# Cross-attention with image prompts: context transposed by VectorE in squares of 32, prompt keys as four columns behind the text keys

## The chip, the cores and the metric

The kernel runs on one core of a Trainium2 chip. TensorE (PE) multiplies, VectorE (DVE) and ScalarE (ACT) read TensorE's results out of PSUM, GpSimd (POOL) works on SBUF, and SyncE (SP) issues most DMAs. The metric is the device time of one execution in microseconds; less is better. All data are float32.

## What is computed

Eight batches, each with S = 112 query rows of 320 channels (20 heads of 16) and a context of 375 rows of 512 embedding values. The first 371 rows are text tokens, the last 4 are image prompt tokens. Cut to what matters:

```python
q   = heads(x @ W_q)                       # 112 x 16 for each of 20 heads
k_t = heads(text @ W_k);  v_t = heads(text @ W_v)
probs_t  = softmax(q k_t^T * 0.25)          # 112 x 371
text_out = probs_t v_t
k_ip = heads(ip @ W_k_ip); v_ip = heads(ip @ W_v_ip)
attn = q k_ip^T * 0.25                      # 112 x 4, the prompt logits
qsem = l2norm(probs_t text)                 # 112 x 512 for each head
sem  = qsem l2norm(ip)^T                    # 112 x 4
probs_ip = softmax(attn + 0.5 * sem) * mask
out = (text_out + probs_ip v_ip) @ W_out + b_out + x
```

The kernel does not form qsem. It uses the Gram matrix of the context: with p the unnormalised probabilities of a head, p (text text^T) p^T gives the norm, and p (text ip^T) the similarities. So for each head it multiplies p by a matrix that has the Gram columns of the 371 text tokens, then 4 columns for the prompts, a column of ones and the 16 value columns: 392 columns in all.

## The kernel before

**Steps.** The 20 heads of a batch are five groups of four. The main loop runs over 40 steps (b,g), batch b and group g. The order of work on TensorE, VectorE, ScalarE and SP is the order of the program text, written out by hand; GpSimd's is left to a scheduler (it is in text order too in the last batch). Within step n:

- `multiplied` (L631): 12 blocks of 32 tokens, each with 4 matmuls (one for a head, in the four row groups of the array) into four PSUM banks ps_qd; since the Gram matrix is symmetric each block is 32 columns narrower than the one before, 392 down to 40.
- `scores` (L584) of step n + 2 (LEAD = 2): two heads after the first block, two after the seventh. They lie in the two PSUM banks ps_s of the pool ps_sc.
- `probabilities` of step n + 2: the row maximum on VectorE (L597, nmx), the exponential on ScalarE (L601, p), and a DMA that puts p into the tile xg (L604).
- `transposed` of step n + 1, after block 2: one VectorE instruction that transposes xg in squares of 32 (L612, xgT). `multiplied` of the next step reads xgT.
- behind the last block: `value_sums` on ScalarE (L644), the maxima of the last two heads, `reduced` on VectorE (L677, four reductions that read the four ps_qd banks), `placed` on GpSimd (L553, value columns into the matrix u of the next step), and then `between`.

**Work between steps.** `between(b, g)` prepares batch b + 1 (and the context of b + 2) a piece at a time: `gram` at g = 0 (L411), `values` at g = 1 and 2 (L480), `keys` block 0 at g = 2 and blocks 1 and 2 at g = 3 (L447; block 2 is a transpose of columns that came with the values, L438), `project_queries` of a pair of batches (x transposed at L295, matmuls L303, then qm = query times a mask on VectorE L312, and qT = a plain copy on ScalarE L315), `finish` of batch b - 1 in ten pieces.

**The context.** `load_ctx` fetches 375 x 512 into the tile ct, token by partition, in four DMAs (L129, L131), at the end of step (b,0) for batch b + 2. `transposed_context` turns it in `between(b, 4)` for batch b + 2: 12 TensorE transposes (L353) into ps_c and three ScalarE copies (L363) into ctxT, which holds embedding by partition and is read by `gram`, `values` and `keys`. The embedding index is e * 128 + p: chunk e, partition p. The weights W_k, W_v, W_k_ip and W_v_ip are loaded in the same order by `load_embed` (L115).

**The prompts' logits.** `prompt_projections` makes kip (keys of all 32 prompt tokens) and from it kipb (L256), each key once for every head of its block with the other heads' channels at zero, for all batches. `prompt_logits(b)` multiplies qT by kipb (L564, three matmuls) in `between(b, 3)`, for the last batch after its step 0, and ScalarE copies the result to ipl (L571), which `finish` reads (L746).

Of the kernel before, what the change touches and what calls it, by code (L numbers as in the profile page):

```python
# [8 lines left out]
F32 = mybir.dt.float32  # L9
# [5 lines left out]
NIP = 4  # L15
# [5 lines left out]
def kernel(  # L21
# [34 lines left out]
    SCALE = D ** -0.5  # L56
    N = B * NIP

    GROUP = 4
    NG = H // GROUP  # L60
    BLK = TP // RG
# [50 lines left out]
        eng.dma_start(t[:REST, FULL, :C], w[FULL * P :, :])  # L112

    def load_embed(eng, t, w):
        eng.dma_start(t[:, :, :C], w.rearrange("(e p) f -> p e f", p=P))  # L115

    def spread(eng, t):

# [2 lines left out]
            eng.tensor_copy(v[:, :, a, 0, :], v[:, :, a // 2, a % 2, :])  # L121
        eng.memset(v[:, :, :, 1, :], 0.0)

    def load_ctx(b):
        ct = io.tile([P, NT, E], F32, tag="ct", name=f"ct_{b}")
        for c in range(NT):
            rows = min(P, T - c * P)
            some = rows - rows % 16
            nc.sync.dma_start(ct[:some, c, :], ehs[b, c * P : c * P + some, :])  # L129
            if some < rows:  # L130
                nc.sync.dma_start(ct[some:rows, c, :], ehs[b, c * P + some : c * P + rows, :])  # L131
        return ct
# [62 lines left out]
    kipb = const.tile([P, NC, B, HC, NIP], F32, tag="kipb", name="kipb")  # L195
# [17 lines left out]
    def normalised_prompts():  # L213

        sq = work.tile([N, E], F32, tag="ipn", name="ipsq", bufs=1)
        ss = small.tile([N, 1], F32, tag="ipss", name="ipss", bufs=1)
        nc.vector.tensor_tensor_reduce(
            out=sq, in0=ip_sb, in1=ip_sb, scale=1.0, scalar=0.0, op0=ALU.mult, op1=ALU.add,
            accum_out=ss,
        )  # L220
        nc.vector.tensor_scalar_max(ss, ss, EPS * EPS)
        rn = small.tile([N, 1], F32, tag="iprn", name="iprn", bufs=1)
        nc.scalar.activation(rn, ss, AF.Sqrt)
        nc.vector.reciprocal(rn, rn)

        ipn = work.tile([N, E], F32, tag="ipn", name="ipn", bufs=1)
        nc.vector.tensor_scalar(ipn, ip_sb, rn, 0.5, op0=ALU.mult, op1=ALU.mult)
        yield

        for src, dst, n in ((ipn, ipnT, "n"), (ip_sb, ipT, "r")):  # L230
            ps = bank(f"ps_ipT{n}")
            for e in range(NE):
                nc.tensor.transpose(
                    ps[:, e * N : (e + 1) * N], src[:, e * P : (e + 1) * P], ident[:N, :N]
                )
            nc.vector.tensor_copy(
                dst, ps[:, : NE * N].rearrange("p (e n) -> p e n", n=N)
            )
        yield

    def prompt_projections():

        spread(nc.gpsimd, wkip_sb)
        for i in range(NC):
            ps = bank(f"ps_kip{i}")
            for e in range(NE):
                nc.tensor.matmul(
                    ps[:, :N],
                    wkip_sb[:, e, i * P : (i + 1) * P],
                    ipT[:, e, :],  # L250
                    start=(e == 0),
                    stop=(e == NE - 1),
                )
            kip = work.tile([P, N], F32, tag="kip", name=f"kip_{i}")
            nc.scalar.copy(kip, ps[:, :N])
            nc.vector.tensor_tensor(  # L256
                kipb[:, i],
                kip.rearrange("p (b n) -> p b n", n=NIP).unsqueeze(2).to_broadcast([P, B, HC, NIP]),
                hmask.unsqueeze(1).unsqueeze(3).to_broadcast([P, B, HC, NIP]),
                ALU.mult,  # L260
            )
# [17 lines left out]
    def project_queries(bs):  # L279
        n = len(bs)  # L280
        xT = work.tile([P, NC, 2 * S], F32, tag="xT", name=f"xT_{bs[0]}", bufs=1)
        qT = work.tile([P, NC, 2 * S], F32, tag="qT", name=f"qT_{bs[0]}", bufs=2)
        qm = work.tile([P, NC, 2, 2 * S], F32, tag="qm", name=f"qm_{bs[0]}", bufs=2)
        for j, b in enumerate(bs):
            queries[b] = (qT, qm, j)
        nc.gpsimd.memset(xT[REST:, FULL, :], 0.0)
# [13 lines left out]
        for i in range(NC):  # L300
            ps = bank(f"ps_q_{bs[0]}_{i}")
            for j in range(NC):
                nc.tensor.matmul(  # L303
                    ps[:, : n * S],
                    wq_sb[:, j, i * P : (i + 1) * P],
                    xT[:, j, : n * S],
                    start=(j == 0),
                    stop=(j == NC - 1),
                )

            for r in range(2 if i < FULL else 1):
                nc.vector.tensor_scalar_mul(  # L312
                    qm[:, i, r, : n * S], ps[:, : n * S], emask[:, r : r + 1]
                )
            nc.scalar.copy(qT[:, i, : n * S], ps[:, : n * S])  # L315
            yield


# [6 lines left out]
    def begin(b):  # L325
        s = st[b] = dict(ct=loaded.pop(b))
        s["ctxT"] = work.tile([P, NE, TP], F32, tag="ctxT", name=f"ctxT_{b}")
        nc.gpsimd.memset(s["ctxT"][:, :, T:], 0.0)
        s["kT"] = work.tile([P, NC, TT], F32, tag="kT", name=f"kT_{b}")
# [15 lines left out]
    def transposed_context(b):  # L345
        begin(b)
        s = st[b]
        ct, ctxT = s["ct"], s["ctxT"]
        for c in range(NT):
            rows = min(P, TT - c * P)  # L350
            ps = bank(f"ps_c_{b}_{c}", spare=b > 1 and c > 0)
            for e in range(NE):
                nc.tensor.transpose(  # L353
                    ps[:, e * P : e * P + rows],
                    ct[:rows, c, e * P : (e + 1) * P],
                    ident[:rows, :rows],
                )
# [71 lines left out]

    def keys(b):  # L430
        s = st[b]
        for i in range(NC):
            ps = bank(f"ps_k_{b}_{i}")
            if 0 < b < B - 1 and i == FULL:

                for c in range(NT):
# [6 lines left out]
                nc.scalar.copy(s["kT"][:, i, :], ps[:, :TT])  # L443
                yield
                return
            for e in range(NE):
# [4 lines left out]
                    start=(e == 0),  # L451
                    stop=(e == NE - 1),
                )
            nc.scalar.copy(s["kT"][:, i, :], ps[:, :TT])  # L454
            yield

    def last_keys(b, ps):

        s = st[b]
        for e in range(NE):  # L460
# [6 lines left out]
                start=(e == 0),  # L467
                stop=(e == NE - 1),
            )
        nc.scalar.copy(s["kT"][:, FULL, :], ps[:, :TT])  # L470
        yield

    def values(b):
# [81 lines left out]
            )  # L555

    def prompt_logits(b):
        s = st[b]
        qT, _, j = queries[b]
        ps = bank(f"ps_ip_{b}")  # L560
        for i in range(NC):
            heads = slice(0, HC, 1) if i < FULL else slice(0, HC, 2)
            hn = min(HC, H - i * HC)
            nc.tensor.matmul(  # L564
                ps[:S, i * HC * NIP : (i * HC + hn) * NIP],
                qT[:, i, j * S : (j + 1) * S],
                kipb[:, i, b, heads, :],
                start=True,
                stop=True,
            )  # L570
# [4 lines left out]
    def scores(b, g, a, early=False, ps=None):  # L575
# [5 lines left out]
            ps = ps_qd.tile([P, 512], F32, tag="qd", name=f"ps_s_{b}_{g}_{a}")  # L581
        elif ps is None:
            ps = ps_sc.tile([P, 512], F32, tag="sc", name=f"ps_s_{b}_{g}_{a}")
        nc.tensor.matmul(  # L584
            ps[:S, :TT],
            qm[a * RG : (a + 1) * RG, i, r, j * S : (j + 1) * S],
            s["kT"][a * RG : (a + 1) * RG, i, :],
            start=True,
            stop=True,
        )  # L590
# [2 lines left out]
    def probabilities(b, g, a):  # L593
# [5 lines left out]
            s["p", g] = work.tile([S, GROUP, TT], F32, tag="p", name=f"p_{b}_{g}", bufs=3)  # L599
        p = s["p", g][:, a, :]  # L600
        nc.scalar.activation(p, ps[:S, :TT], AF.Exp, bias=nmx)  # L601

        xg = x_ring[(b * NG + g) % NX]
        nc.sync.dma_start(  # L604
# [251 lines left out]
            for _ in gen:  # L856
                pass

    LEAD = 2
    steps = [(b, g) for b in range(B) for g in range(NG)]  # L860

    gens = {}
# [8 lines left out]
    def between(b, g):  # L871
# [166 lines left out]
    for g in range(NG):  # L1038
# [30 lines left out]
        if g == 0:  # L1069
            own_channels(bd)  # L1070
            with_bias(b)
            drain(prompt_logits(b))
            run(("f", b - 2), None)
        if g == 1:
            prompt_values(b)
# [77 lines left out]
```

## Time and profile before

| What | Value |
|---|---|
| median of three runs | 450.31 us (450.1 to 450.73) |
| the profiled execution's own time | 450.23 us |
| its span, first to last instruction | 448.5 us |
| granted TensorE clock, mean | 0.998 |
| VectorE, the 40 transposes of xg (L612) | 118.9 us, 2973 ns each |
| VectorE, reductions (L677) and maxima (L597) | 80.2 and 77.5 us |
| ScalarE, exponentials (L601) | 82.4 us |
| DMA, mean rate | 145 GB/s |

The profile is one execution, with the start and end of every instruction. "Busy" is the union of an engine's instructions. The chain of waits is followed back from the last instruction, at each step to what released it. A timeline line gives the start, the length, the engine, the source line, the operation with its output and inputs, and, in brackets, the time that the engine stood idle just before, with what ended it. Groups give the busy time and the mean length of one instruction. Matmuls and the loads of their stationary operands (PEld) are pipelined, so the length of one is longer than its share of the engine; a stretch's cost is read from start to start.

### The profile page before, as it was taken

The numbers are of one execution on the slowest core, as the hardware profiler recorded it, in microseconds if no ns is written. First come the engines' busy times: TensorE is split into PE (matmuls) and PEld (weight loads), VectorE is DVE, ScalarE is ACT, GpSimd is POOL, SyncE is SP. The second block draws the span as 40 slices with busy tenths as digits, with TensorE's granted clock in tenths as the row PEclk, the third lists the DMA queues.
The fourth block names the chain that finished last, engine by engine and source line by source line (L and its number), as shares of the span: only waits on it lengthen the run. The fifth ranks groups of instructions, "written<-read, shape, count | busy, mean of one in ns | idle before, by whom it ended". The sixth has DMA issues, their size and how long they took to land.

```text
span 448.5 us, 12974 instructions
## 1 busy us (share of the span) xinstructions
PE 435.1 (97%) x5137; PEld 336.2 (75%) x5137; DVE 308.2 (69%) x649; ACT 194.1 (43%) x543; POOL 110.0 (25%) x263
## 2 busy tenths in 40 slices
PE   8998999999999999999999999999999999999885
PEld 8756767887778777788777786788777887787682
DVE  4047366786687767686687866776687867878784
ACT  2254233345335353343434453343534353346782
POOL 4302200012050211511142120512123111527430
PEclk9999999999999999999999999999999999999999
DMA  8669964544645565545646366455656437453500
GB/s 243 183 164 252 203 143 140 141 142 143 169 122 130 144 172 163 137 118 142 163 127 158 113 177 162 126 136 143 163 163 144 134 88 190 127 141 103 144 2 26
DMA packets 52158, 64.83 MB, mean 145 GB/s; under 512 B 18370, under 2 KB 44146, under 8 KB 52098
## 3 DMA queue, kind: packets, MB, share of 16 engines
q1 hardware_dynamic: 51658, 63.45, 53.7%
q8 instruction: 40, 0.66, 0.7%
q10 hardware_dynamic: 440, 0.56, 0.4%
q14 instruction: 20, 0.16, 0.1%
HBM read 19.30 MB, written 5.32 MB: 55 GB/s over the span
## 4 chain that ended last, share of the span: by engine, by line
PE 88%; DVE 3%; ACT 3%; DMA 3%; issue 1%; POOL 1%; SPq 1%; DVEq 0%; ACTq 0%
PE ps_qd L631 41%; PE ps_v L480 14%; PE ps_k L447 9%; PE ps_g L411 8%; PE ps_s L584 4%; PE ps_q L303 3%; PE ps_c L353 2%; PE ps_o L848 2%; DMA xg<-p 1%; ACT p L601 1%; PE ps_g L383 1%; DVE junk L677 1%; PE ps_ip L564 1%; DVE xgT L612 1%; PE ps_k L463 1%
## 5 line engine op out<-in xcount | busy, mean ns | idle before, releaser
L631 PE MATMUL ps_qd<-u,xgT 32*112 32x104 f32 (+11 forms) x3840 | 216.6, 352 | 3.6 <-POOL u L553 1.3
L631 PEld LDWEIGHTS ps_qd<-u,xgT 32*112 32x112 f32 x3840 | 182.5, 172 | 38.5 <-issue 9.8
L597 DVE TENSOR_REDUCE nmx<-ps_s 112x1 f32<-112x371 f32 x160 | 77.5, 529 | 73.3 <-PE ps_s L584 73.3
L612 DVE STREAM_TRANSPOSE xgT<-xg 128x1536 f32<-128x1536 f32 x40 | 118.9, 2973 | 8.7 <-DMA xg<-p 7.7
L601 ACT ACTIVATE p<-ps_s,nmx 112x371 f32<-112x371 f32 x160 | 82.4, 572 | 64.5 <-DVE nmx L597 46.7
L677 DVE CUSTOM_DVE_ANT_0 junk<-ps_qd,p 112x371 f32<-112x371 f32 x148 | 80.2, 542 | 15.6
L553 POOL COPY u<-vr 128x64 f32<-128x64 f32 x120 | 26.0, 238 | 169.8 <-PE ps_qd L631 112.5
L584 PE MATMUL ps_s<-kT,qm 32*112 32x371 f32 x320 | 63.5, 476 | 0.6 <-ACT p L601 0.4
L480 PE MATMUL ps_v<-wv_sb,ctxT 128*128 128x384 f32 (+1 forms) x192 | 63.5, 480 | 0.0
L480 PEld LDWEIGHTS ps_v<-wv_sb,ctxT 128*128 128x128 f32 x192 | 35.2, 190 | 19.7
L447 PE MATMUL ps_k<-ctxT,wk_sb 128*128 128x371 f32 x136 | 45.9, 482 | 0.0
L644 ACT COPY pvs<-ps_qd 112x21 f32<-112x21 f32 x150 | 16.1, 189 | 65.7 <-PE ps_qd L631 64.8
L411 PE MATMUL ps_g<-ctxT 128*128 128x375 f32 (+2 forms) x168 | 37.4, 379 | 0.0
L447 PEld LDWEIGHTS ps_k<-ctxT,wk_sb 128*128 128x128 f32 x136 | 25.1, 190 | 15.3 <-issue 0.5
L411 PEld LDWEIGHTS ps_g<-ctxT 128*128 128x128 f32 x168 | 28.1, 190 | 8.4
L584 PEld LDWEIGHTS ps_s<-kT,qm 32*112 32x112 f32 x320 | 25.5, 170 | 6.3 <-ACT kT L454 2.0
L312 DVE TENSOR_SCALAR qm<-ps_q,emask 128x224 f32<-128x224 f32 (+1 forms) x25 | 9.2, 400 | 24.5 <-PE ps_q L303 24.5
L487 ACT COPY vext<-ps_v 128x384 f32<-128x384 f32 (+1 forms) x24 | 11.2, 466 | 25.7 <-PE ps_v L480 25.2
L454 ACT COPY kT<-ps_k 128x371 f32<-128x371 f32 x17 | 8.0, 469 | 26.5 <-PE ps_k L447 26.5
L399 ACT ACTIVATE ug<-ps_g 128x375 f32<-128x375 f32 (+2 forms) x24 | 9.0, 377 | 23.5 <-PE ps_g L411 20.5
L817 POOL TENSOR_TENSOR wv<-vip,w 112x1280 f32<-112x1280 f32 x6 | 14.8, 2462 | 14.6 <-DVE w L761 14.6
L400 POOL TENSOR_TENSOR ug<-ug,half 128x128 f32<-128x128 f32 (+1 forms) x24 | 10.7, 450 | 29.9 <-ACT ug L399 29.9
(129 smaller groups left out, 336.1 us busy)
## 6 DMA issues: line engine op xcount, KB each, us to landing
xg<-p SPq DMA_DIRECT2D x160, 162.3 KB
u<-ug SPq DMA_DIRECT2D x128, 99.0 KB
ct<-in_ctx_dram SPq DMA_DIRECT2D x16, 256.0 KB
vip<-vipd SPq DMA_DIRECT2D x7, 560.0 KB
vr<-vd SPq DMA_DIRECT2D x32, 120.0 KB
vd<-vext SPq DMA_DIRECT2D x7, 320.0 KB
ct<-in_ctx_dram SPq DMA_DIRECT2D x8, 224.0 KB
vd<-vext SPq DMA_DIRECT2D x7, 160.0 KB
```

The costliest lines, as they stand in the source:

```text
L411: nc.tensor.matmul(ps[:, : T - t0], ctxT[:, e, t0 : t0 + P], ctxT[:, e, t0:T], start=(e == 0), stop=(e == NE - 1),)
L447: nc.tensor.matmul(ps[:, :TT], wk_sb[:, e, i * P : (i + 1) * P], s["ctxT"][:, e, :TT], start=(e == 0), stop=(e == NE - 1),)
L480: nc.tensor.matmul(ps[:, :w], ctxT[:, e, c * P : (c + 1) * P], wv_sb[:, e, :w], start=(e == 0), stop=(e == NE - 1),)
L553: nc.gpsimd.tensor_copy(region(b, c)[:, :, UV - c * P :], s["vr"][:, c * QN : (c + 1) * QN, g, :])
L584: nc.tensor.matmul(ps[:S, :TT], qm[a * RG : (a + 1) * RG, i, r, j * S : (j + 1) * S], s["kT"][a * RG : (a + 1) * RG, i, :], start=True, st ...
L597: nc.vector.tensor_reduce(nmx, ps[:S, :TT], AX.X, ALU.max, negate=True)
L601: nc.scalar.activation(p, ps[:S, :TT], AF.Exp, bias=nmx)
L612: nc.vector.transpose(xT.rearrange("p j (k q) -> p q j k", q=QN), xg.rearrange("p q (j k) -> p q j k", k=RG),)
L631: nc.tensor.matmul(banks[a][:S, j * RG : UW], xT[a * RG : (a + 1) * RG, j, :S], region(b, c)[a * RG : (a + 1) * RG, q, q * RG :], start=(j ...
L644: nc.scalar.copy(s["pvs"][:, h, :], ps[:S, TT:UW])
L677: nc.vector.tensor_tensor_reduce(out=junk, in0=ps[:S, :TT], in1=s["p", g][:, a, :], scale=1.0, scalar=0.0, op0=ALU.mult, op1=ALU.add, accu ...
L817: eng.tensor_tensor(wv, s["vip"][:, :, part], w.rearrange("p h n -> p n h").unsqueeze(3).to_broadcast([S, NIP, n, D]), ALU.mult,)
```

## The change

Four things change together.

1. *Context.* For batches from LEAD = 2 on, `load_ctx` puts 32 tokens on each quarter of the partitions: quarter a holds the embedding values a * 128 to a * 128 + 127 of token 32 j + i at partition 32 a + i, block j. That takes four DMAs for the 11 full blocks, four for the last 19 tokens, and a GpSimd clearing of the last block. `transposed_context` is then three VectorE transposes, each of 128 partitions by 512 values in squares of 32, straight into ctxT. The prompt rows are no longer loaded with the context. Contexts 0 and 1 are still turned by TensorE.
2. *Order of the embedding.* Partition p, chunk e now holds value 4 p + e. `load_embed` loads the weights so, and the TensorE transposes of contexts 0 and 1 and of the prompts read every fourth value (`chunk`).
3. *Prompt keys.* For b > 0 the tile kT has 375 columns; GpSimd copies the batch's four columns of kip behind the 371 text keys, each score matmul has 375 columns, and ScalarE copies the last four of each head to ipl behind the exponential. `prompt_logits` and kipb remain for batch 0 alone, as does qT.
4. *Places.* The context's transposes stand at the end of `between(b, 1)` (one) and `between(b, 3)` (two); key block 2 moves from `between(b, 3)` to `between(b, 4)`.

```diff
     def load_embed(eng, t, w):
-        eng.dma_start(t[:, :, :C], w.rearrange("(e p) f -> p e f", p=P))
+        eng.dma_start(t[:, :, :C], w.rearrange("(p e) f -> p e f", e=NE))
...
+    def chunk(t, e):
+        return t.rearrange("t (p e) -> t e p", e=NE)[:, e, :]
...
     def load_ctx(b):
         ct = io.tile([P, NT, E], F32, tag="ct", name=f"ct_{b}")
+        if b >= LEAD:
+            v = ct.rearrange("p c e -> p (c e)").rearrange("p (j f) -> p j f", f=P)
+            full = TT // RG
+            nc.gpsimd.memset(v[:, full, :], 0.0)
+            for a in range(QN):
+                nc.sync.dma_start(
+                    v[a * RG : (a + 1) * RG, :full, :],
+                    ehs[b, : full * RG, a * P : (a + 1) * P].rearrange("(j i) f -> i j f", i=RG),
+                )
+            for a in range(QN):
+                nc.sync.dma_start(
+                    v[a * RG : a * RG + TT - full * RG, full, :],
+                    ehs[b, full * RG : TT, a * P : (a + 1) * P],
+                )
+            return v
...
     def transposed_context(b):
...
+        if b >= LEAD:
+            for c in range(NT):
+                some = slice(c * QN, (c + 1) * QN)
+                nc.vector.transpose(
+                    ctxT[:, :, c * P : (c + 1) * P].rearrange("p e (j i) -> p j e i", i=RG),
+                    ct[:, some, :].rearrange("p j (k e) -> p j e k", e=NE),
+                )
+                yield
+            return
...
-                    ct[:rows, c, e * P : (e + 1) * P],
+                    chunk(ct[:, c, :], e)[:rows],
...
     def keys(b):
         s = st[b]
+        if b > 0:
+            nc.gpsimd.tensor_copy(s["kT"][:, :, TT:], kip[:, :, b * NIP : (b + 1) * NIP])
...
     def scores(b, g, a, early=False, ps=None):
...
+        w = T if b > 0 else TT
         nc.tensor.matmul(
-            ps[:S, :TT],
+            ps[:S, :w],
             qm[a * RG : (a + 1) * RG, i, r, j * S : (j + 1) * S],
-            s["kT"][a * RG : (a + 1) * RG, i, :],
+            s["kT"][a * RG : (a + 1) * RG, i, :w],
...
     def probabilities(b, g, a):
...
         nc.scalar.activation(p, ps[:S, :TT], AF.Exp, bias=nmx)
+        if b > 0:
+            nc.scalar.copy(s["ipl"][:, groups[g][a], :], ps[:S, TT:T])
...
     def between(b, g):
...
-            run(("t", b), lambda: prompt_logits(b))
-            if nb < B - 1:
-                run(("k", nb), None, 1)
+            if b == 0:
+                run(("t", b), lambda: prompt_logits(b))
...
+        if g in (1, 3) and nb + 1 < B:
+            run(("c", nb + 1), lambda: transposed_context(nb + 1), g // 2 + 1)
         if g == 4:
-            if nb + 1 < B:
-                run(("c", nb + 1), lambda: transposed_context(nb + 1))
             if b > 0 and new:
                 run(("f", b - 1), None, 2)
-            if nb + 1 < B:
-                run(("c", nb + 1), None, 2)
+            if nb < B - 1:
+                run(("k", nb), None, 1)
```

More of the change, by code (lines that the diff above doesn't have):

```diff
@@ L57 @@
     N = B * NIP
+    LEAD = 2
     GROUP = 4
@@ L194 @@
     ipnT = const.tile([P, NE, N], F32, tag="ipnT", name="ipnT")
-    kipb = const.tile([P, NC, B, HC, NIP], F32, tag="kipb", name="kipb")
+    kip = const.tile([P, NC, N], F32, tag="kip", name="kip")
+    kipb = const.tile([P, NC, HC, NIP], F32, tag="kipb", name="kipb")
     vipd = dram.tile([N, C], F32, tag="vipd", name="vipd", bufs=1)
@@ L233, in normalised_prompts @@
                 nc.tensor.transpose(
-                    ps[:, e * N : (e + 1) * N], src[:, e * P : (e + 1) * P], ident[:N, :N]
+                    ps[:, e * N : (e + 1) * N], chunk(src, e), ident[:N, :N]
                 )
@@ L253, in prompt_projections @@
                 )
-            kip = work.tile([P, N], F32, tag="kip", name=f"kip_{i}")
-            nc.scalar.copy(kip, ps[:, :N])
+            nc.scalar.copy(kip[:, i, :], ps[:, :N])
             nc.vector.tensor_tensor(
                 kipb[:, i],
-                kip.rearrange("p (b n) -> p b n", n=NIP).unsqueeze(2).to_broadcast([P, B, HC, NIP]),
-                hmask.unsqueeze(1).unsqueeze(3).to_broadcast([P, B, HC, NIP]),
+                kip[:, i, :NIP].unsqueeze(1).to_broadcast([P, HC, NIP]),
+                hmask.unsqueeze(2).to_broadcast([P, HC, NIP]),
                 ALU.mult,
@@ L281, in project_queries @@
         xT = work.tile([P, NC, 2 * S], F32, tag="xT", name=f"xT_{bs[0]}", bufs=1)
-        qT = work.tile([P, NC, 2 * S], F32, tag="qT", name=f"qT_{bs[0]}", bufs=2)
         qm = work.tile([P, NC, 2, 2 * S], F32, tag="qm", name=f"qm_{bs[0]}", bufs=2)
+        qT = const.tile([P, NC, S], F32, tag="qT", name="qT") if bs[0] == 0 else None
         for j, b in enumerate(bs):
@@ L314, in project_queries @@
                 )
-            nc.scalar.copy(qT[:, i, : n * S], ps[:, : n * S])
+            if qT is not None:
+                nc.scalar.copy(qT[:, i, :], ps[:, :S])
             yield
@@ L327, in begin @@
         s["ctxT"] = work.tile([P, NE, TP], F32, tag="ctxT", name=f"ctxT_{b}")
-        nc.gpsimd.memset(s["ctxT"][:, :, T:], 0.0)
-        s["kT"] = work.tile([P, NC, TT], F32, tag="kT", name=f"kT_{b}")
+        if b < LEAD:
+            nc.gpsimd.memset(s["ctxT"][:, :, T:], 0.0)
+        s["kT"] = work.tile([P, NC, T], F32, tag="kT", name=f"kT_{b}")
         s["vext"] = work.tile([P, NT, C + REST], F32, tag="vext", name=f"vext_{b}", bufs=1)
@@ L348, in transposed_context @@
         ct, ctxT = s["ct"], s["ctxT"]
+        if b >= LEAD:
[7 more added lines that the diff above has]
+            return
         for c in range(NT):
             rows = min(P, TT - c * P)
-            ps = bank(f"ps_c_{b}_{c}", spare=b > 1 and c > 0)
+            ps = bank(f"ps_c_{b}_{c}")
             for e in range(NE):
@@ L442, in keys @@
                     )
-                nc.scalar.copy(s["kT"][:, i, :], ps[:, :TT])
+                nc.scalar.copy(s["kT"][:, i, :TT], ps[:, :TT])
                 yield
@@ L453, in keys @@
                 )
-            nc.scalar.copy(s["kT"][:, i, :], ps[:, :TT])
+            nc.scalar.copy(s["kT"][:, i, :TT], ps[:, :TT])
             yield
@@ L469, in last_keys @@
             )
-        nc.scalar.copy(s["kT"][:, FULL, :], ps[:, :TT])
+        nc.scalar.copy(s["kT"][:, FULL, :TT], ps[:, :TT])
         yield
@@ L558, in prompt_logits @@
         s = st[b]
-        qT, _, j = queries[b]
+        qT = queries[b][0]
         ps = bank(f"ps_ip_{b}")
@@ L565, in prompt_logits @@
                 ps[:S, i * HC * NIP : (i * HC + hn) * NIP],
-                qT[:, i, j * S : (j + 1) * S],
-                kipb[:, i, b, heads, :],
+                qT[:, i, :],
+                kipb[:, i, heads, :],
                 start=True,
@@ L857, in drain @@
                 pass
-    LEAD = 2
     steps = [(b, g) for b in range(B) for g in range(NG)]
@@ L1071 @@
             with_bias(b)
-            drain(prompt_logits(b))
             run(("f", b - 2), None)
```

## The prediction

> **What bounds the kernel.** I read the page's engine line first, then the chain of waits, then the timelines of TensorE and VectorE over two neighbouring steps. A step is one pass of the main loop, written (b,g): batch b, group g of four heads.
>
> ```profile
> PE 435.1 (97%) x5137; PEld 336.2 (75%) x5137; DVE 308.2 (69%) x649; ACT 194.1 (43%) x543; POOL 110.0 (25%) x263
> PE 88%; DVE 3%; ACT 3%; DMA 3%; issue 1%; POOL 1%; SPq 1%; DVEq 0%; ACTq 0%
> ```
>
> TensorE is busy 97% of the span and makes 88% of the chain, so work taken off it is worth its whole length until another engine is late. The chain of waits gives the step starts (first ps_qd matmul): batch 1 at 94.58, 105.43, 116.15, 126.77, 136.80; batch 2 at 146.35, 156.97, 167.69, 178.31, 188.96; batch 3 at 198.49. So g = 0 to 2 take 10.6 to 10.9 us, g = 3 takes 10.0 (odd b) or 10.65 (even b), g = 4 takes 9.5. The change edits only what stands behind g = 3 and g = 4. TensorE's timeline at the end of (2,3), through (2,4):
>
> ```profile
> 186.19 0.67 PE L564 MATMUL ps_ip<-kipb,qT 128*112 128x32 f32 x6
> 187.01 0.51 PE L438 MATMUL ps_k<-ident,k 128*128 128x128 f32 x3
> 187.35 0.45 PE L835 MATMUL ps_a<-ident,attn 112*128 112x112 f32 x3
> 187.64 1.31 PE L303 MATMUL ps_q<-xT,wq_sb 128*128 128x224 f32 x6
> 188.89 1.22 PE L631 MATMUL ps_qd<-u,xgT 32*112 32x392 f32 x10
> ...
> 192.79 0.48 PE L584 MATMUL ps_s<-kT,qm 32*112 32x371 f32 x2
> ...
> 194.24 0.66 PE L353 MATMUL ps_c<-ident,ct 128*128 128x128 f32 x4
> 194.74 1.78 PE L848 MATMUL ps_o<-wo_sb,aT 128*112 128x320 f32 x6
> 196.35 1.00 PE L353 MATMUL ps_c<-ident,ct 128*128 128x128 f32 x8
> 197.18 1.31 PE L303 MATMUL ps_q<-xT,wq_sb 128*128 128x224 f32 x6
> 198.42 1.22 PE L631 MATMUL ps_qd<-u,xgT 32*112 32x392 f32 x10
> ```
>
> Columns: start, length, engine, line. There is no gap; the context's transposes (L353) and the prompt logits (L564) lie bare on the bound. VectorE beside it:
>
> ```profile
> 186.50 0.55 DVE L677 CUSTOM_DVE_ANT_0 junk<-ps_qd,p 112x371 f32<-112x371 f32 x1
> 186.97 0.08 DVE L677 DVE_READ_ACCUMULATOR2_ANT ss<- 112x1 f32 x1
> 189.00 0.81 DVE L312 TENSOR_SCALAR qm<-ps_q,emask 128x224 f32<-128x224 f32 x2 [1.94 <-PE ps_q L303]
> 190.47 0.99 DVE L597 TENSOR_REDUCE nmx<-ps_s 112x1 f32<-112x371 f32 x2 [0.66 <-PE ps_s L584]
> 191.38 2.95 DVE L612 STREAM_TRANSPOSE xgT<-xg 128x1536 f32<-128x1536 f32 x1
> 194.17 0.94 DVE L597 TENSOR_REDUCE nmx<-ps_s 112x1 f32<-112x371 f32 x2
> 195.03 0.53 DVE L677 CUSTOM_DVE_ANT_0 junk<-ps_qd,p 112x371 f32<-112x371 f32 x1
> ```
>
> Here is the second limit. In each step VectorE must do, in order, two maxima (nmx), the 2.95 us transpose, two maxima and four reductions (junk). The first nmx waits for scores, 1.5 us after the step's start; from it to the last junk's end is 7.2 us (190.47 to 197.66). The next step's fourth ps_qd bank is that junk's bank, so **no step can be much shorter than 1.5 + 7.1 = 8.7 us**. Batch 0 shows the edge: (0,4) took 8.59 us, its last junk ending at 94.7 and the next step starting at 94.58. The same nmx also gates TensorE inside a step: the last two scores (192.79) reuse the two ps_s banks that the first two exponentials free.
>
> **Removed from TensorE.** Context transposes: 0.50 (194.24 to 194.74) + 0.83 (196.35 to 197.18) = 1.33 us for each of six contexts, 8.0 us. Prompt logits: 186.19 to about 186.9, with the keys' transpose held until 187.01; the chain gives 0.74. They go in seven batches: some 5 us. In (b,3) the third key block (L438, 0.34 to 0.5 us) also leaves, to return in (b,4).
>
> **Added to TensorE.** Scores of b > 0 get 375 columns for 371. The ps_qd rows fall from 462 ns at 360 columns to 328 ns at 200: 0.84 ns a column, so 4 x 0.84 x 280 records = 0.9 us.
>
> **Added to VectorE.** Three transposes of 128x512 per context, one behind (b,1), two behind (b,3), each ahead of the next step's nmx. The trace has no 32x32 transpose that reads at a step of four words; the nearest row, L612, writes at that step: 2973 ns for 1536, or 0.99 us for 512, about 0.95 in sequence. Bounds: a dense read at the nmx rate (529 ns for 371) gives 0.7, 0.6 at the least; a read that halves the rate, 1.9. I take 0.95, since L612 moves the same blocks and differs only in which side is strided. The Trainium skill speaks against the move twice. "VectorE: DVE Perf Modes", section "Rules for kernel authors", sends a transpose of 128x128 to TensorE, and its section "The three transpose paths" has 311 ns for VectorE in bf16: four such are an estimated 1.24 us per 128x512. The row is shorter, and the layout here needs only squares of 32. The page "SBUF — State Buffer", section "Door 1: The DMA port swizzle", says that reads which enter a new 16-byte line each time pay a penalty. L612 pays at most that on its writes; no run here shows reads. By the 1.24 the sum below is 3 us worse, by a doubled rate 11 us.
>
> **Step by step.**
> - (b,1): VectorE idles 2.94 us ahead of the next nmx (210.63, [2.94 <-PE ps_s]). One transpose fits: nothing.
> - (b,3): TensorE saves 1.0 us (ps_a and ps_q start a microsecond sooner): 9.0 odd, 9.65 even. Both above 8.7.
> - (b,4), odd b: junk ends 8.7 after the start of (b,3), two transposes take it to 10.65; nmx could run at 9.0 + 1.5 = 10.5. Late by 0.15. TensorE needs 9.55 - 1.33 + 0.5 = 8.7, VectorE 8.75: 8.8. Saves 0.75; in b = 5, whose (b,4) took 9.07, 0.3.
> - (b,4), b = 2 and 4: ahead of the transposes stand two qm scalings, which wait for ps_q, the last matmul of the stretch. They end 0.9 after the step's start, the transposes 2.8: nmx is late by 1.3. The last score of the step then waits too (behind nmx come 0.63 and two exponentials with their copies, 1.25: free at 4.7, wanted at 3.85), and the step lasts 2.8 + 7.1 = 9.9. Costs 0.4.
> - b = 0: (0,3) keeps its logits, saves 0.35; (0,4) goes from 8.59 to 9.9. Costs 1.0 in all.
> - b = 6: no context; 0.7 saved in (6,3). b = 7: the logits (0.69 on the chain) go, some 0.2 returns as copies between the last exponentials: 0.5.
>
> Sum: -1.75 x 2 - 1.3 - 0.6 x 2 + 1.0 - 0.7 - 0.5 + 0.9 = **-5.3 us**. TensorE gives up 12 and gets 5 back, because (b,4) becomes VectorE's.
>
> **At nothing.** ScalarE gains 140 copies of 112x4; four like them (pvs, L644) take 0.41 together, 0.1 each, and it loses the ctxT, qT and ipl copies. Put between exponentials they hold a ps_s bank 0.2 us longer; the slack is 0.67 (139.97 to 140.64 in (1,4)), so without nmx's delay they are free. GpSimd's key copy (384 elements, about 0.2) goes behind one u copy and ahead of the 2.46 us wv, with 3 us until the scores; behind wv's group (2.46 + 1.55 + 2 x 0.86 us) it would hold the scores of (b,3) by 2 to 3 us. SP issues eight context loads for four. At 0.42 us each (L129 median) they run from 207.2 to 210.8; xg at 211.86 is next. Were each the longest seen, 0.97, xg would be 3 us late, but its transpose comes a step later. The last four wait for GpSimd to clear the tail of ct, and xg would stand behind them; GpSimd is idle then. The loads land in pieces of 512 bytes; first use is a step later, where it was four. If they are late, VectorE stands at the transpose behind (b,1), and nmx, the exponentials and xg behind it; the 2.94 us of idle time and some 7 us between landing and use cover that. The weights' rows (p e) change order, not bytes. In the prologue, contexts 0 and 1 and the prompts enter the weight load at a step of four words (L353, 141 ns): between 0 and a doubling, 12 x 0.14 = 1.7 us on the path; I take 0.3, since the first load waits mostly for DMA and scalar copies.
>
> 450.23 (profiled; span 448.5 and 1.7 around it) - 5.3 + 0.3 = **445.2**. The median, 450.31, is 0.1 higher: 445.3.
>
> **Rivals.**
> 1. *The strided read halves VectorE's rate* (ends slower). Two transposes cost 1.9 us more. Even b and 0: +1.9 x 3; odd: nmx late by 2.05, +1.8 x 3: 11 us, so **456**. It decides from about 1.4 us per 128x512, where the 5 us are used up. For it: the cacheline rule. Against: L612 is no slower per element than its writes allow, 1.94 ns. Chance 0.14.
> 2. *Cheap transposes*: at 0.6 each, nmx is 0.6 late in even b; 0.75 x 3 + 0.3 more: **442.5**. Were VectorE to hide all, TensorE's 12 us would give 438; the 8.7 us edge speaks against. Chance 0.19.
> 3. *All given back* (about 1.3 us each, or xg late as steps shorten; its DMA already ended four VectorE waits, 7.7 us): **450**. Chance 0.07.
> 4. The forecast, 443.5 to 448.5: 0.55. Remaining 0.05: slower for a reason not listed, such as the GpSimd clearing of ct waiting.
>
> Changes under 0.2% (449.4 to 451.2) cannot be told from none. Range 441.5 to 452.5. Faster 0.74, same 0.07, slower 0.19.
>
> **What would show it.** 128x512 transposes near 1 us; (b,3) at 9.0 and 9.65; (b,4) at 8.8 odd and 9.9 even, with nmx late behind the transposes in even batches and TensorE stalled ahead of its last ps_s; (b,0) to (b,2) unchanged. A transpose of 1.4 us or more, or a ps_qd start waiting for ct, would make me wrong.

## The result, and the profile after

The changed kernel took **451.06 us** (median of 12 runs, 449.04 to 452.15), the kernel before beside it 450.71 us (12 runs, 449.83 to 451.76). The ratio is 1.0003, its 95% interval 0.999 to 1.0016: no difference that can be measured, where 5 us less had been forecast. The profiled execution has a span of 449.5 us, 1.0 more than before, at a granted clock of 0.998 as before.

The engine line of the page after:

```profile
PE 432.3 (96%) x5023; PEld 331.9 (74%) x5023; DVE 326.2 (73%) x667; ACT 188.2 (42%) x646; POOL 112.1 (25%) x270
```

TensorE has 114 matmuls less, but its busy time fell by only 2.8 us and its share by one point. VectorE's busy time rose by 18.0 us. The work moved as planned; what TensorE no longer does became time in which it waits. Part of that waiting lies inside the records of its matmuls and counts as busy: the same 3840 ps_qd matmuls make 222.7 us on the page after and 216.6 on the page before. Where TensorE waits, the timeline of the same stretch shows, the end of (2,3) through (2,4):

```profile
187.49 0.45 PE L877 MATMUL ps_a<-ident,attn 112*128 112x112 f32 x3
187.78 1.31 PE L326 MATMUL ps_q<-xT,wq_sb 128*128 128x224 f32 x6
189.02 1.22 PE L673 MATMUL ps_qd<-u,xgT 32*112 32x392 f32 x10
...
193.06 0.56 PE L624 MATMUL ps_s<-kT,qm 32*112 32x375 f32 x1
193.08 0.33 PE L673 MATMUL ps_qd<-u,xgT 32*112 32x200 f32 x2
193.47 0.68 PE L624 MATMUL ps_s<-kT,qm 32*112 32x375 f32 x2
...
195.44 1.87 PE L890 MATMUL ps_o<-wo_sb,aT 128*112 128x320 f32 x6
197.14 0.48 PE L476 MATMUL ps_k<-ident,k 128*128 128x128 f32 x3
198.19 1.40 PE L326 MATMUL ps_q<-xT,wq_sb 128*128 128x224 f32 x6 [0.56 <-ACT kT L481]
199.52 0.93 PE L673 MATMUL ps_qd<-u,xgT 32*112 32x392 f32 x8
```

The logits and the context's transposes are gone. The step is longer all the same, 10.50 us (189.02 to 199.52) for 9.54, and for two reasons. The last four scores are spread from 193.06 on, with a few ps_qd matmuls between them: the 12 blocks take 6.49 us from the start of the first ps_qd to the end of the last, where they took 5.42 before. What they wait for stands at the load of the stationary operand of one of these scores; ScalarE must first have read the bank:

```profile
193.58 0.17 PEld L624 LDWEIGHTS ps_s<-kT,qm 32*112 32x112 f32 x1 [0.26 <-ACT ipl L643]
```

And ps_q stands [0.56 <-ACT kT], a wait that the timeline before did not have. VectorE beside it:

```profile
189.13 0.81 DVE L335 TENSOR_SCALAR qm<-ps_q,emask 128x224 f32<-128x224 f32 x2 [0.75 <-PE ps_q L326]
189.86 2.07 DVE L379 STREAM_TRANSPOSE ctxT<-ct 128x512 f32<-128x512 f32 x2
191.85 0.96 DVE L637 TENSOR_REDUCE nmx<-ps_s 112x1 f32<-112x371 f32 x2
192.72 2.95 DVE L654 STREAM_TRANSPOSE xgT<-xg 128x1536 f32<-128x1536 f32 x1
195.50 0.94 DVE L637 TENSOR_REDUCE nmx<-ps_s 112x1 f32<-112x371 f32 x2
```

The first maximum starts 2.83 us after the step's start instead of 1.58, behind the two context transposes. They take 2.07 together.

Lengths of the steps, from the first ps_qd of one to that of the next, before and after, in us:

| stretch | before | after | difference | forecast |
|---|---|---|---|---|
| to the first ps_qd of (0,0) | 36.34 | 37.14 | +0.8 | +0.3 |
| (0,3) to the end of (1,0) | 29.85 | 30.73 | +0.9 | +1.0 |
| (b,3), b = 1, 3 | 10.03 | 9.68 | -0.35 each | -1.0 |
| (b,4), b = 1, 3 | 9.55 | 9.44 | -0.1 each | -0.75 |
| (b,3), b = 2, 4 | 10.65 | 9.50 | -1.15 each | -1.0 |
| (b,4), b = 2, 4 | 9.54 | 10.50 | +0.96 each | +0.4 |
| (5,3) to the end of (6,0) | 29.71 | 30.52 | +0.8 | -1.3 |
| (6,3) | 9.56 | 9.01 | -0.55 | -0.7 |
| batch 7 | | | +0.1 | -0.5 |
| wider scores, all other steps | | | +0.25 | +0.9 |

The differences add up to the 1.0 us by which the span grew. The largest misses are batches 1 and 3 (2.6 us together) and batch 5 (2.1 us).

### The profile page after: what moved, and what is told of

It is laid out like the page before. It is cut to its first block, busy times and chain, and to the rows that moved or that the text cites. A ratio compares the mean times of both kernels' runs of the same rounds, so it can differ in the third digit from the quotient of the medians.

```text
span 449.5 us, 12968 instructions
## 1 busy us (share of the span) xinstructions
PE 432.3 (96%) x5023; PEld 331.9 (74%) x5023; DVE 326.2 (73%) x667; ACT 188.2 (42%) x646; POOL 112.1 (25%) x270
## 5 line engine op out<-in xcount | busy, mean ns | idle before, releaser
L673 PE MATMUL ps_qd<-u,xgT 32*112 32x104 f32 (+11 forms) x3840 | 222.7, 353 | 3.2 <-DVE xgT L654 1.3
L673 PEld LDWEIGHTS ps_qd<-u,xgT 32*112 32x112 f32 x3840 | 187.8, 172 | 38.5 <-issue 9.8
L654 DVE STREAM_TRANSPOSE xgT<-xg 128x1536 f32<-128x1536 f32 x40 | 119.1, 2977 | 9.4 <-DMA xg<-p 7.9
L641 ACT ACTIVATE p<-ps_s,nmx 112x371 f32<-112x371 f32 x160 | 86.9, 582 | 92.7 <-DVE nmx L637 67.4
L624 PE MATMUL ps_s<-kT,qm 32*112 32x375 f32 (+1 forms) x320 | 67.7, 483 | 0.4 <-ACT p L641 0.3
L624 PEld LDWEIGHTS ps_s<-kT,qm 32*112 32x112 f32 x320 | 26.9, 170 | 6.6 <-ACT kT L492 2.1
L643 ACT COPY ipl<-ps_s 112x4 f32<-112x4 f32 x140 | 23.6, 168 | 0.0
L326 PE MATMUL ps_q<-xT,wq_sb 128*128 128x224 f32 (+1 forms) x90 | 17.4, 329 | 3.2 <-ACT kT L481 3.1
L379 DVE STREAM_TRANSPOSE ctxT<-ct 128x512 f32<-128x512 f32 x18 | 19.0, 1082 | 0.0
```

Source lines behind the costliest of these rows:

```text
L379: nc.vector.transpose(ctxT[:, :, c * P : (c + 1) * P].rearrange("p e (j i) -> p j e i", i=RG), ct[:, some, :].rearrange("p j (k e) -> p j ...
L624: nc.tensor.matmul(ps[:S, :w], qm[a * RG : (a + 1) * RG, i, r, j * S : (j + 1) * S], s["kT"][a * RG : (a + 1) * RG, i, :w], start=True, st ...
L643: nc.scalar.copy(s["ipl"][:, groups[g][a], :], ps[:S, TT:T])
L654: nc.vector.transpose(xT.rearrange("p j (k q) -> p q j k", q=QN), xg.rearrange("p q (j k) -> p q j k", k=RG),)
L673: nc.tensor.matmul(banks[a][:S, j * RG : UW], xT[a * RG : (a + 1) * RG, j, :S], region(b, c)[a * RG : (a + 1) * RG, q, q * RG :], start=(j ...
```

## The experiments

**What stands in the odd batches.** The timeline of TensorE after, the end of (1,3) and the end of (1,4):

```profile
136.37 0.74 PE L318 MATMUL ps_x<-ident,x_sb 112*128 112x112 f32 x6
137.68 0.48 PE L877 MATMUL ps_a<-ident,attn 112*128 112x112 f32 x3 [0.57 <-ACT xT L321]
138.09 1.22 PE L673 MATMUL ps_qd<-u,xgT 32*112 32x392 f32 x10
...
145.16 0.48 PE L476 MATMUL ps_k<-ident,k 128*128 128x128 f32 x3
146.20 1.40 PE L326 MATMUL ps_q<-xT,wq_sb 128*128 128x224 f32 x6 [0.56 <-ACT kT L481]
147.53 0.93 PE L673 MATMUL ps_qd<-u,xgT 32*112 32x392 f32 x8
```

What holds the two banks of ps_mm at that moment, from the timelines of ScalarE and of VectorE in the same run:

```profile
145.68 0.47 ACT L481 COPY kT<-ps_k 128x371 f32<-128x371 f32 x1 [0.62 <-PE ps_k L476]
```

```profile
146.80 0.48 DVE L850 TENSOR_TENSOR ob<-ps_o,xb 112x320 f32<-112x320 f32 x1
```

One bank has ps_o until VectorE has read it at 147.28; the other has the moved key block until ScalarE has copied it at 146.15. The query projection needs a bank and starts at 146.20. Before, the last context transposes stood between ps_o and ps_q, and no key block. Whether it is the transposes that are missing there or the block that is one too many, the run with the key block put back tells below. In (1,3) banks of the pool ps_sc hold TensorE: the last two of the three ps_x blocks and ps_a take its two banks, and ps_a starts when ScalarE's xT copies are done. Before, the prompt logits and the key block stood between them, and ps_a had no wait:

```profile
134.66 0.74 PE L295 MATMUL ps_x<-ident,x_sb 112*128 112x112 f32 x6
135.38 0.76 PE L564 MATMUL ps_ip<-kipb,qT 128*112 128x32 f32 x6
135.99 0.52 PE L438 MATMUL ps_k<-ident,k 128*128 128x128 f32 x3
136.35 0.45 PE L835 MATMUL ps_a<-ident,attn 112*128 112x112 f32 x3
```

Hence two theories. M: matrix-work banks that come free late hold TensorE in (b,4). V: the context's transposes hold VectorE's maxima in the even batches.

**e1_spare_bank: key block 2 in a bank of the score pool** (M alone):

```diff
-            ps = bank(f"ps_k_{b}_{i}")
-            if 0 < b < B - 1 and i == FULL:
+            late = 0 < b < B - 1 and i == FULL
+            ps = bank(f"ps_k_{b}_{i}", spare=late and b > 1)
+            if late:
```

> The changed kernel, with the third key block of batches 2 to 6 in a bank of the pool ps_sc, where it no longer shares the two ps_mm banks with the query projection. Theory V (VectorE alone sets the length of (b,4)): nothing moves, within 0.3 us. Theory M (behind the moved key block TensorE waits 0.56 us for ScalarE to empty the key block's bank, because ps_o holds the other one until VectorE's last reduction is done): the wait ahead of ps_q goes in (1,4) to (4,4), odd (b,4) from 9.44 to about 8.85, even from 10.50 to about 9.95, some 2.1 us in all.

Measured: 448.76 us (448.61 to 449.31), 0.994 of the kernel before [0.9917, 0.9964]. (1,4) and (3,4) went from 9.44 to 8.63, (2,4) and (4,4) from 10.50 to 9.69: the bank's wait costs **0.81 us** in each (from ps_k to ps_q 1.04 us pass where 0.32 do without the wait, as the next but one experiment shows, and 0.09 more behind ps_q). Of this the step that follows, (b + 1,0), gives back 0.2 behind odd and about 0.3 behind even batches; it lasts 10.84 and 10.96 instead of 10.63. M is shown.

**e2_early_transposes: the context's transposes ahead of the steps with room** (V; two behind (b,1), one behind (b,2)):

```diff
-        if g in (1, 3) and nb + 1 < B:
-            run(("c", nb + 1), lambda: transposed_context(nb + 1), g // 2 + 1)
+        if g in (1, 2) and nb + 1 < B:
+            run(("c", nb + 1), lambda: transposed_context(nb + 1), 3 - g)
```

> The changed kernel, with the context's three VectorE transposes moved: two behind (b,1), one behind (b,2), none behind (b,3). VectorE's idle time ahead of the next nmx is 2.9 us and 1.25 us there, and the transposes take 2.08 and 1.08. Theory V: (b,4) falls to VectorE's own limit of 8.8 everywhere, 7 to 8 us in all. Theory V with M: even (b,4) falls from 10.50 only to the 9.44 of odd batches, (0,4) with (1,0) loses 1.3, (5,4) with (6,0) 1.4: about 5 us. If VectorE's delay were not what costs in even batches: nothing.

Measured: 446.91 us (445.89 to 448.43), ratio 0.99 [0.9867, 0.9933]. (2,4) and (4,4) fell to 9.44, exactly the odd batches' value: VectorE's delay is gone there and the bank's wait is left. So the 10.50 us are a sum: 8.63 of work, 0.81 of bank wait, 1.06 of scores that wait behind late exponentials. Batch 0 gained 0.5 and batch 5 nothing, less than expected: in (5,3) VectorE stood 2.09 us for a late xg, for 1.00 in the changed kernel, and the step took 10.38 for 9.50.

**e3_all_three: both, and for odd batches ps_a in the other pool:**

```diff
-        ps = bank(f"ps_a_{b}_{h0}", spare=not late)
+        ps = bank(f"ps_a_{b}_{h0}", spare=not late and b % 2 == 1)
```

> Early transposes and spare bank together, and in odd batches the bank of ps_a taken from ps_mm instead of ps_sc (in (1,3) and (3,3) TensorE waits 0.57 us for ScalarE's copy of xT out of that ps_sc bank). V with M: (b,3) 9.1 in odd batches, (b,4) about 8.8 in all, 9 us less than the changed kernel, so some 442 us. V alone: no more than the early transposes alone give. M alone: no more than the spare bank gives.

Measured: **443.83 us** (443.19 to 444.68), ratio 0.983 [0.9805, 0.9855]. This version is faster than both kernels, by 1.7% against the kernel before. TensorE's timeline of the same two places:

```profile
136.44 0.74 PE L318 MATMUL ps_x<-ident,x_sb 112*128 112x112 f32 x6
137.25 0.48 PE L878 MATMUL ps_a<-ident,attn 112*128 112x112 f32 x3
137.66 1.22 PE L674 MATMUL ps_qd<-u,xgT 32*112 32x392 f32 x10
...
144.73 0.48 PE L477 MATMUL ps_k<-ident,k 128*128 128x128 f32 x3
145.05 1.31 PE L326 MATMUL ps_q<-xT,wq_sb 128*128 128x224 f32 x6
146.29 1.14 PE L674 MATMUL ps_qd<-u,xgT 32*112 32x392 f32 x8
```

No brackets: from ps_x to ps_a 0.81 us instead of 1.31, from ps_k to ps_q 0.32 instead of 1.04. (1,3) is 9.19 us long, (1,4) and (2,4) 8.63.

**e5_prompt_keys_alone** (the kernel before, with part 3 of the change and nothing else; its core):

```diff
+            nc.gpsimd.tensor_copy(s["kT"][:, :, TT:], kip[:, :, b * NIP : (b + 1) * NIP])
...
-            run(("t", b), lambda: prompt_logits(b))
+            if b == 0:
+                run(("t", b), lambda: prompt_logits(b))
```

> The kernel before with part 3 of the change alone: prompt keys as four columns, prompt logits gone for b > 0; contexts, embedding order and places as before. Theory M (in the changed kernel the two removals of TensorE work in odd (b,3) leave a hole that waits for ScalarE): here the key block's transpose stays in (b,3) and fills the hole, so (b,3) is 0.6 to 0.75 us shorter in batches 1 to 6, the 375 columns cost 0.01 us a step, and the kernel is 3.5 to 4 us faster than before, about 446.7, so faster than the whole change. Rival (the logits were hidden anyway): within 0.5 us of before.

Measured: 447.81 us (446.6 to 448.29), ratio 0.994 [0.992, 0.996]. This part of the change is worth 2.6 us by itself; the rest of the change, put on top of it, takes as much back. In the odd batches (b,3) is 9.68 here too. Key block 2 still stood in (b,3), so in odd batches its departure gained nothing in the changed kernel: ps_a waits for the xT copies with it or without it. The expected 0.6 to 0.75 us of these steps were 0.35.

**e6_key_block_back: key block 2 back in (b,3)** of the changed kernel:

```diff
+            if nb < B - 1:
+                run(("k", nb), None, 1)
...
-            if nb < B - 1:
-                run(("k", nb), None, 1)
```

> The changed kernel with one place undone: the third key block stays in (b,3). M: the wait ahead of ps_q in (b,4) goes. Odd: (b,3) stays at 9.7 (the block fills the hole), (b,4) 8.65 with 0.2 given back in the next step. Even: (b,3) 9.5 to about 9.9, (b,4) 10.50 to 9.7. Some 2.5 us less than the changed kernel, near the run with the spare bank. V alone: nothing in (b,4), 0.3 to 0.4 us more in each (b,3).

Measured: 449.57 us (20 runs, 448.01 to 451.93), ratio 0.998 [0.9966, 0.9994]; that is 1.5 us below the changed kernel, where 2.5 had been expected. TensorE's timeline at the end of (1,4):

```profile
143.77 1.87 PE L890 MATMUL ps_o<-wo_sb,aT 128*112 128x320 f32 x6
145.47 1.30 PE L326 MATMUL ps_q<-xT,wq_sb 128*128 128x224 f32 x6
146.70 1.22 PE L673 MATMUL ps_qd<-u,xgT 32*112 32x392 f32 x9
```

Here ps_q follows ps_o without a wait, though the context's transposes are gone from between them as well. So it was not as a filler that they were missed: the block is one too many. In the odd (b,4) it costs 9.44 - 8.30 = 1.14 us, of which 8.63 - 8.30 = 0.33 are its matmuls and 0.81 the wait for its bank. Odd batches: (b,4) 8.30 and (b + 1,0) 11.17, together 19.47, as with the spare bank; (b,3) unchanged. Even batches: (b,3) 10.02, (b,4) 9.41 and (b + 1,0) 11.23, together 30.66 for 30.63, no gain. Two quite different kernels thus meet the same floor; a step can end sooner, but the next one pays. In odd batches (b,4) plus what (b + 1,0) has over 10.63 makes 8.30 + 0.54 = 8.84 here and 8.63 + 0.21 = 8.84 there; in even ones 9.41 + 0.60 = 10.01 and 9.69 + 0.33 = 10.02. That floor ought to be VectorE's: the last junk frees the fourth ps_qd bank. The run e9 below tests it.

**e8 and e9: dense writes in VectorE's large transpose**, once in the changed kernel (e8) and once in e3_all_three (e9):

```diff
-            xT.rearrange("p j (k q) -> p q j k", q=QN),
+            xT.rearrange("p j (q k) -> p q j k", q=QN),
```

> The changed kernel with one line different: the transpose of xg (L654) writes its squares side by side (dense) where it wrote at a step of four words; the columns of xgT then stand in another order than the kernel needs, and the padding of xg is one for zero, so the output differs from the reference. Nothing else moves. If the strided side costs on writes what it cost on reads (1.85 against 1.11 ns an element), L654 falls from 2977 to some 1850 ns. Theory (VectorE's chain is the edge in the even (b,4), 20.6 us for (b,4) + (b,0) with no bank wait, and the wait for a ps_mm bank is the bound in the odd ones): even sums fall from 21.13 to about 20.1, odd sums stay at 20.07, batch 0 gains up to 0.6; 2 to 3 us less than the changed kernel, so 448 to 449. Rival (the two maxima held by the context's transposes alone set the even steps, L654 comes after them): nothing changes, 451. Other rival: writes pay no penalty, L654 stays at 2977 ns.

> The kernel of e3_all_three with the same line different (dense writes of xgT; columns in another order and padding of one, so the output differs from the reference). Theory: in e3 nothing but VectorE's edge (8.7 us) is left behind (b,4), which gives 0.2 back in (b,0) (10.84 against 10.63). With L654 at 1850 ns the edge is at 7.6 and these 0.2 go, in five batches: 1.0 to 1.5 us less than e3's 443.83, so 442.5. If (b,0) stays at 10.84, the 0.2 are not VectorE's but TensorE's own work, and the time is e3's.

(The 1.85 ns an element are an estimate: 1082 ns for 512 and 2977 for 1536 elements a partition differ by 1895 ns for 1024.) Measured in the changed kernel: 447.59 us (447.55 to 448.3), ratio 0.9937 [0.9922, 0.9952]. The group of the transpose:

```profile
L654 DVE STREAM_TRANSPOSE xgT<-xg 128x1536 f32<-128x1536 f32 x40 | 70.8, 1769 | 9.8 <-DMA xg<-p 7.0 <-DMA vd<-vext 1.6 <-DMA ct<-in_ctx_dram 1.0
```

1769 ns for 2977: the writes at a step of four words were 1.2 us of each of the 40. VectorE's timeline in (2,4):

```profile
188.54 2.08 DVE L379 STREAM_TRANSPOSE ctxT<-ct 128x512 f32<-128x512 f32 x2
190.54 0.96 DVE L637 TENSOR_REDUCE nmx<-ps_s 112x1 f32<-112x371 f32 x2
191.41 1.77 DVE L654 STREAM_TRANSPOSE xgT<-xg 128x1536 f32<-128x1536 f32 x1
```

The transpose is shorter, but the first maximum is as late as before, and (2,4) is still 10.50 us. The expectation that even sums fall to 20.1 missed, and for these steps the rival held: the stall in the even batches comes from the two context transposes ahead of the maximum and from the bank, not from the chain as a whole. That the time came out next to the theory's 448 to 449 all the same, and not at the rival's 451, is mostly luck, since of the steps that the theory named only batch 0 gained. In the profiled pair the span is 3.7 us shorter, by (1,0) (0.7), batch 5 with (6,0) (1.35), the last batch (1.0) and the start (0.6, a stretch that differs by as much between other kernels).

In e3_all_three: 440.61 us (439.38 to 441.31), ratio 0.9784 [0.9767, 0.98], 3.2 us below its twin with strided writes, where 1.0 to 1.5 had been expected. (2,0) to (5,0) fell from 10.84, 10.84, 10.90 and 11.07 to 10.63 each, so these 0.2 to 0.4 us are VectorE's. The end of (2,4), first the version with strided writes, VectorE and TensorE, then the one with dense writes:

```profile
196.24 0.54 DVE L720 CUSTOM_DVE_ANT_0 junk<-ps_qd,p 112x371 f32<-112x371 f32 x1
```

```profile
196.62 1.22 PE L674 MATMUL ps_qd<-u,xgT 32*112 32x392 f32 x10
```

```profile
192.96 0.54 DVE L720 CUSTOM_DVE_ANT_0 junk<-ps_qd,p 112x371 f32<-112x371 f32 x1
```

```profile
193.83 1.22 PE L674 MATMUL ps_qd<-u,xgT 32*112 32x392 f32 x10
```

With strided writes the last junk ends at 196.78, after the next step has begun at 196.62; with dense ones it ends at 193.50, 0.33 ahead. Beside this 1.1 us the profiled pair differs by 0.5 in (1,0), 1.35 from (5,3) to (6,4), 0.2 in batch 7, 0.4 at the start and 1.7 in (0,0). This last is one profiled execution's: from 37.0 to 52.9 us the version with strided writes had a granted clock of 0.91, the other 1.00, and the medians show it in part at most.

**e7_dense_reads: dense reads in the context's transposes:**

```diff
-                    ct[:, some, :].rearrange("p j (k e) -> p j e k", e=NE),
+                    ct[:, some, :].rearrange("p j (e k) -> p j e k", e=NE),
```

> The changed kernel, with VectorE's context transposes reading 32 neighbouring columns instead of every fourth (the channels of ctxT then stand in another order than the weights' rows, so the result differs from the reference). If the strided read costs nothing: 1.08 us each as before, and 449 to 451 us. If it costs: shorter, down to 0.6 us, and even (b,4) shorter by twice the difference.

One run, 447.81 us, so without an interval. The group of these transposes, first after, then here:

```profile
L379 DVE STREAM_TRANSPOSE ctxT<-ct 128x512 f32<-128x512 f32 x18 | 19.0, 1082 | 0.0
```

```profile
L379 DVE STREAM_TRANSPOSE ctxT<-ct 128x512 f32<-128x512 f32 x18 | 12.0, 693 | 0.0
```

The strided read costs 0.39 us of 1.08. The maximum in (2,4) starts 2.05 after the step's start instead of 2.83, and the step falls from 10.50 to 9.72: 0.78 for 0.78 saved on VectorE. So in the even batches what the pair ahead of nmx takes counts in full.

**e4_dense_weights: dense loads of TensorE's stationary operand** (for the 0.8 us at the start):

```diff
-        return t.rearrange("t (p e) -> t e p", e=NE)[:, e, :]
+        return t[:, e * P : (e + 1) * P]
```

> The changed kernel, with TensorE's transposes of contexts 0 and 1 and of the prompts reading 128 neighbouring columns again (their channels then stand in another order than the weights' rows, so the result differs from the reference). If the strided load of the stationary operand is what makes the prologue 0.8 us longer (217 ns a load against 141): the first ps_qd starts at 36.3 instead of 37.1, 0.8 us less in all. If it is the weights' new loading order or the new DMAs: still 37.1.

Measured: 450.31 us (20 runs, 448.13 to 452.88), ratio 0.9994 [0.9979, 1.0008]. The loads of operands of 115 rows and 128 columns took 212 ns each after and 140 here, so the load itself is dearer at that step. But the first ps_qd, which was to come at 36.3 us, came at 37.78, later than the 37.14 of the changed kernel. The first exponential came at 26.45 us for 27.09 after; but other kernels with the strided loads had it at 26.43 to 27.01, and their first ps_qd at 36.27 to 37.15. So it is not shown that the loads make the start later, nor that the 0.8 us of the table are more than scatter.

## Why the prediction was wrong

**The step that failed: "(b,4), odd b: ... TensorE needs 9.55 - 1.33 + 0.5 = 8.7, VectorE 8.75: 8.8".** The sum of work was right: 8.63 once no bank is missing. VectorE's limit was right: the floor is 8.84 (forecast 8.7 to 8.8), and 10.0 in even batches (9.9). But the step counted TensorE's work as if every matmul could start when the one before it was done. The moved key block stands in this sum with its 0.5 us of matmul; it took 0.33, but it also takes one of the two ps_mm banks while ps_o has the other, and ps_q behind it waits until ScalarE has emptied the block's bank. The block's true cost there was 1.14 us. The wait is 0.81 us on TensorE, 0.6 net of VectorE's floor in odd batches and 0.5 in even ones, 2.2 us in the four steps. The forecast missed the profiled execution by 6.0 us (-5.0 with the start, +1.0 measured); ps_a's wait, next, makes 1.0 of them and batch 5 makes 2.1, and the rest is smaller terms of both signs.

**"(b,3): TensorE saves 1.0 us ... 9.0 odd".** It saved 0.35, since a bank is waited for in the other pool too: ps_a waits for the xT copies. What left the step had covered them, so here the removed work was filler, and the key block's leaving gained nothing. With ps_a in a bank of ps_mm the step takes 9.19. Even batches have no ps_x and took 9.50 (forecast 9.65). In batches 1 and 3 the forecast for both steps was 17.8 us; the changed kernel took 19.12, and the version with free banks 17.82, of which the next step gives 0.2 back.

**"b = 2 and 4: ... nmx is late by 1.3. The last score of the step then waits too."** Right: late by 1.25, 1.06 of stall, in the place that was named. The forecast took the larger of VectorE's and TensorE's limits; the stall inside TensorE's stream adds to TensorE's own work and to the bank's wait, 8.63 + 1.06 + 0.81 = 10.50.

**The size of a transpose.** 0.95 us in sequence was taken, 1.04 was measured (2.07 for two). The argument was that the row L612 bounds the penalty, since it pays it on its writes. It does, and the penalty in that row is large: 1.2 of its 2.98 us. The page "SBUF — State Buffer" of the Trainium skill, section "Door 1: The DMA port swizzle", was right that accesses that enter a new 16-byte line each time pay: 1082 against 693 ns on reads and 2977 against 1769 ns on writes. No run tried another step than four words, so that it is the line that counts is not shown here. The rule pointed the right way, and the row, which shows the penalty already paid, gave the right size; the 1.24 us estimated from the figure for bf16 were above even the strided 1.08. Nor does the skill's page "VectorE: DVE Perf Modes", section "Rules for kernel authors", speak against the move as the prediction has it: it sends a transpose of 128x128 to TensorE, but its next row calls VectorE's transpose the fastest for squares of 32, and this layout needs no more than those. Moved to steps with room, with the banks sorted out, they bring the kernel to 443.83 us, against 447.81 for the prompt keys alone, with the contexts still on TensorE; part of these 4.0 us is ps_a's bank, which was not tried with the contexts on TensorE.

**Batch 5**, forecast -1.3, measured +0.8. VectorE's timeline of (5,3) and (5,4) after:

```profile
338.20 2.99 DVE L654 STREAM_TRANSPOSE xgT<-xg 128x1536 f32<-128x1536 f32 x1 [1.00 <-DMA xg<-p]
...
344.44 2.08 DVE L379 STREAM_TRANSPOSE ctxT<-ct 128x512 f32<-128x512 f32 x2
346.44 0.94 DVE L637 TENSOR_REDUCE nmx<-ps_s 112x1 f32<-112x371 f32 x2
```

And before:

```profile
337.51 2.98 DVE L612 STREAM_TRANSPOSE xgT<-xg 128x1536 f32<-128x1536 f32 x1 [0.86 <-DMA vd<-vext]
...
345.67 0.99 DVE L597 TENSOR_REDUCE nmx<-ps_s 112x1 f32<-112x371 f32 x2 [1.85 <-PE ps_s L584]
```

The transpose of xg waited for a DMA in the trace before too, 0.86 us, and it cost nothing, since VectorE then had 1.85 us of idle time ahead of the maximum in (5,4). The context's transposes fill that idle time: the maximum stands right behind them, 0.74 late. The forecast for b = 5 took VectorE's end in (5,3) as that of an undisturbed step, 8.7 us after the start; it was 9.9, and the trace before already had 9.75. This is read from the traces, not tested alone: the wait in (5,3) runs from 0.04 us (prompt keys alone) to 2.09 (early transposes) between kernels, and why the DMA lands late stays open.

**Smaller terms.** Batch 0 (+1.0 forecast, +0.9) and b = 6 (-0.7, -0.55) were right, though in batch 0 the delay came a step later than forecast: (0,4) fell to 8.09, and (1,0) rose from 10.85 to 12.58. In batch 7 the logits' 0.69 us were no gain: a key matmul now waits [0.62 <-ACT shared], so they had covered ScalarE. The wider scores cost 0.25 us where 0.9 was taken from the pitch of ps_qd columns. GpSimd's key copy (0.19 us; it has 1536 elements, not the 384 of the prediction), the eight context loads and ScalarE's 140 copies cost nothing that a step shows.

Of the rivals, "all given back", at 450, was nearest in size. Its mechanisms, dearer transposes or a late xg, are only a part: 0.1 us a transpose, and batch 5.

## What to carry to other kernels

Work on the critical engine is worth its length only if what follows could start that much sooner. Before subtracting it, list what each later matmul waits for, its PSUM bank above all, who empties that bank and when: work that covered such a wait leaves it bare when it goes. A piece that is moved brings its bank with it, and where the next matmul needs that bank the wait can cost more than the piece itself, here 0.81 us beside 0.33. When work moves to an engine with idle time, ask which instruction of the critical engine is queued behind it, and put it where that instruction has slack: the same three transposes cost some 4 us (medians) in one place, and in the other the steps behind them did not grow. A row that serves as a yardstick may already contain the penalty in question; the dense form of the same instruction settles it.

## What was not expected of the hardware

VectorE's transpose in squares of 32 takes 1769 ns for 128x1536 float32 values when both sides are dense and 2977 ns when it writes at a step of 16 bytes; for 128x512, 693 and 1082 ns with the step on the reads. TensorE's load of a stationary operand of 115 rows and 128 columns took 212 ns at that step and 140 dense, with no effect on the time that could be told from scatter.
